# Decoder: six bf16 matmuls of ones in each step and five before the first, whose results nothing reads

## The chip, the cores and the metric

The kernel runs on one core of one Trainium2 chip. The metric is the device time of one execution in microseconds. Three runs of the kernel before took 1675.52, 1684.32 and 1690.44 us (median 1684.32).

## The reference

The program is a chain of eight blocks on an activation `x` of 16 sequences of 64 tokens with 128 features, each adding its result to `x`: an attention decoder with a recurrent cell, three mixture-of-experts blocks, a perceiver, a quantised feed-forward, six transformer layers and one transformer block. The change touches the first one only, the decoder. For each of the 16 sequences, with the normalised tokens as inputs and `cond_1024` as the first hidden state, it computes over 64 steps

```
def step(carry, x):
    h, stopped = carry
    stop = jnp.logical_or(stopped, jnp.mean(x) == 0)
    logits = jnp.concatenate([x, h]) @ W_attn.T + b_attn
    aw = jax.nn.softmax(logits)
    applied = aw @ enc
    comb = jax.nn.relu(jnp.concatenate([x, applied]) @ W_comb.T + b_comb)
    h_new = jnp.tanh(comb @ W_ih.T + b_ih + h @ W_hh.T + b_hh)
    out = h_new @ W_out.T + b_out
```

A step needs the hidden state of the step before it, so the 64 steps cannot be taken in parallel.

## The kernel before

**Layout.** Features stand on the 128 partitions; the 16 sequences are the 16 columns of a step's operands. Whatever does not depend on the hidden state is computed for all steps ahead of the loop (the prologue, L1525 to L1555): `XL`, `XC` and `HX` are the inputs' parts of the logits, of the combination and of the recurrent sum, and `E2` is the context already multiplied by the combination's weights.

**One step** (the loop at L1559) is written in the order in which it runs; the planner that orders other stages is switched off here, so each engine's queue has the order of the source. TensorE works as follows, all in float32:

- `lg`: the step's logits, started by a matmul with the identity that brings in `XL`, and finished by `mm4` with the hidden state. `mm4` (L1334) splits one matmul into four, each of which fills 32 of the array's columns, a column tile. ScalarE takes the exponential into `bd` (L1568).
- `hh`: the recurrent sum, started by an identity matmul that brings in `HX`, continued by `mm4` with `whh` and the old hidden state.
- `su`: the sums of the softmax, `mm4` with ones; VectorE takes the reciprocal.
- `cb`: eight `mm4` of two columns each, the attention applied to `E2`; VectorE multiplies by the reciprocal and takes a maximum, which gives `co` (L1581, L1582).
- `hh` is finished by `mm4` with `wih` and `co`; ScalarE takes the tanh into the next hidden state (L1584).

The identity matmuls of the next step, for `lg` and for `hh`, are issued in this step, ahead of the work on `co` and behind the finishing of `hh`. VectorE gets, at the end of each step, some operations of a list called `todo` (an exact test for inputs of zero mean), which nothing in the loop waits for. PSUM holds two buffers each of `su`, `cb`, `lg` and `hh`, of 16 columns. A float32 matmul stands in the trace as two records, so an `mm4` is eight.

**Matmuls of ones.** `self.units` is a bf16 tile of ones (L1325), and `fill` (L1328) issues n matmuls of it into a PSUM tile that is free. Other stages' planner calls it to keep TensorE occupied; the decoder of the kernel before does not call it. A line in a profile is that of the helper which issues: L296 is every matmul (`mm`), so groups are told apart by tile. After the loop 16 matmuls with `wout` give the block's output (tile `pj` from `H`).

**Around it.** While the prologue and the first steps run, SyncE's queue loads weights of the next stage (`m_sb`, 4 MB in parts), which arrive until about 28.6 us after the span's start. The decoder's steps lie between about 20 and 224.5 us.

Of the kernel before, what the change touches and what calls it, by code (L numbers as in the profile page):

```python
# [13 lines left out]
AF = mybir.ActivationFunctionType  # L14
# [1127 lines left out]
class _Plan:  # L1142
# [122 lines left out]
    def run(self, tries=1, fill=None, banks=()):  # L1265

        for o in reversed(self.ops):
            o.tail = o.ns + max(
                (u.tail + (self.hop(o, u) if full else -o.ns) for u, full in o.users), default=0)
        best = None  # L1270
        for seed in range(tries):
            rng = random.Random(seed)
            shift = {}
            out = self.order(lambda o: 1.0 + (rng.random() - 0.5) * 0.02 * min(seed, 1))
            if out is not None and (best is None or out[-1][1] < best[-1][1]):
                best = out
        fills = self.fills(best, banks) if fill else {}
        for _, _, o, s in best:
            if o.k in fills:
                n, (kind, k) = fills[o.k]  # L1280
                fill(self.kinds[kind][0][k], n)
            if o.takes is not None:
                o.slot = (s, self.kinds[o.takes][0][s])
            o.emit(o.home.slot and o.home.slot[1])
        self.ops = []
        return best


class _Fast(_Net):
# [35 lines left out]
        self.units = self.const.tile([128, 512], BF16, tag="units", name="units")  # L1325
        nc.gpsimd.memset(self.units, 1.0)

    def fill(self, t, n):  # L1328

        t = t[:, 0, :] if len(t.shape) == 3 else t  # L1330
        for _ in range(n):
            self.mm(t, self.units[:, :128], self.units)

    def mm4(self, out, lhsT, rhs, start=True, stop=True):  # L1334

# [174 lines left out]
    def decoder(self):  # L1510
        nc, tc = self.nc, self.tc
        w = self.w0
        x = self.x
        with ExitStack() as st:
            pool = st.enter_context(tc.tile_pool(name="d_sb", bufs=1))
            full = lambda tag: self.tile(pool, [128, B, T], tag)
            H, lnT, XL, XC, HX, RR = (full(k) for k in ("H", "lnT", "XL", "XC", "HX", "RR"))
            E2 = self.tile(pool, [128, NT, D], "E2")
            keep, zero = self.tile(pool, [128, NT], "keep"), self.tile(pool, [128, NT], "zero")
            ones = self.tile(pool, [128, 128], "ones")  # L1520
            nc.gpsimd.memset(ones, 1.0)
            bsum, lbias = self.tile(pool, [128, 1], "bsum"), self.tile(pool, [128, B], "lbias")
            todo = self.exact_zero(pool, x, zero)
            with tc.tile_pool(name="d_ps", bufs=4, space=PSUM) as ps, tc.manual_schedule(engines=None):
                ln = self.tile(pool, [128, NT, D], "ln")  # L1525
                flat = lambda a, h: a[:, h * 8:(h + 1) * 8, :].rearrange("p b t -> p (b t)")
                ctxT = full("ctxT")
                for h in range(2):
                    self.norm_half(x, h, ln[:, h * 4:(h + 1) * 4, :])
                self.to_features(ps, self.ctx, lambda h, t: nc.vector.tensor_copy(flat(ctxT, h), t))  # L1530
                self.to_features(ps, ln, lambda h, t: nc.scalar.copy(flat(lnT, h), t))

                nc.vector.tensor_scalar(lbias, self.c("half16"), -NEG, NEG, ALU.mult, ALU.add)
                nc.vector.tensor_scalar(lbias, lbias, w("battn2"), None, ALU.add)
                nc.vector.tensor_tensor(bsum, w("bih"), w("bhh"), ALU.add)
                for h in range(2):
                    t = self.tile(ps, [128, 512], "pj")
                    self.mm(t, w("wcx"), flat(lnT, h))
                    nc.vector.tensor_scalar(flat(XC, h), t, w("bcomb"), -1.0, ALU.add, ALU.mult)
                for h in range(2):  # L1540
                    t = self.tile(ps, [128, 512], "pj")
                    self.mm(t, w("wax2"), flat(lnT, h))
                    nc.vector.tensor_tensor(
                        XL[:, h * 8:(h + 1) * 8, :], t.rearrange("p (b t) -> p b t", t=T),
                        lbias[:, h * 8:(h + 1) * 8].unsqueeze(2).to_broadcast([128, 8, T]), ALU.add)
                for h in range(2):
                    t = self.tile(ps, [128, 512], "pj")
                    self.mm(t, w("wih"), flat(XC, h))
                    nc.scalar.activation(flat(HX, h), t, AF.Identity, bias=bsum, scale=-1.0)
                for h in range(2):  # L1550
                    t = self.tile(ps, [128, 4, 128], "pj")
                    for k in range(4):
                        i = h * 4 + k
                        self.mm(t[:, k, :], ctxT[:, 2 * i:2 * i + 2, :].rearrange("p b t -> p (b t)"), w("wca"))
                    self.evac(h, E2[:, h * 4:(h + 1) * 4, :], t)  # L1555

            with tc.tile_pool(name="d_rs", bufs=2) as rp, tc.tile_pool(name="d_rps", bufs=2, space=PSUM) as ps, \
                    tc.manual_schedule(engines=None):
                for t in range(T):  # L1559
                    h = w("cond") if t == 0 else H[:, :, t - 1]  # L1560
                    su, cb = (self.tile(ps, [128, 16], k) for k in ("su", "cb"))
                    if t == 0:
                        lg, hh = (self.tile(ps, [128, 16], k) for k in ("lg", "hh"))
                    if t == 0:
                        self.mm(lg, self.ident, XL[:, :, t], True, False)
                    self.mm4(lg, w("wah2"), h, False, True)
                    bd = self.tile(rp, [128, 16], "bd")
                    nc.scalar.activation(bd, lg, AF.Exp)  # L1568
                    if t == 0:
                        self.mm(hh, self.ident, HX[:, :, t], True, False)  # L1570
                    self.mm4(hh, w("whh"), h, False, False)
                    self.mm4(su, ones, bd)
                    r = RR[:, :, t]
                    nc.vector.reciprocal(r, su)
                    for c in range(NT):
                        self.mm4(cb[:, 2 * c:2 * c + 2], E2[:, c, :], bd[:, 2 * c:2 * c + 2])
                    if t < T - 1:
                        lg = self.tile(ps, [128, 16], "lg")
                        self.mm(lg, self.ident, XL[:, :, t + 1], True, False)
                    co = self.tile(rp, [128, 16], "co")  # L1580
                    nc.vector.tensor_tensor(co, cb, r, ALU.mult)  # L1581
                    nc.vector.tensor_tensor(co, co, XC[:, :, t], ALU.max)  # L1582
                    self.mm4(hh, w("wih"), co, False, True)
                    nc.scalar.activation(H[:, :, t], hh, AF.Tanh)  # L1584
                    if t < T - 1:
                        hh = self.tile(ps, [128, 16], "hh")
                        self.mm(hh, self.ident, HX[:, :, t + 1], True, False)
                    for _ in range(-(-len(todo) // (T - t))):
                        todo.pop(0)()
            with tc.tile_pool(name="d_ps2", bufs=2, space=PSUM) as ps:  # L1590

                t = self.tile(ps, [128, 512], "pj")
                self.mm(t[:, :NT], self.c("tri"), zero)
                nc.vector.tensor_scalar(keep, t[:, :NT], 0.5, None, ALU.is_lt)
                out = self.new_x()
                for h in range(2):
                    t = self.tile(ps, [128, 4, 128], "pj")
                    for k in range(4):
                        i = h * 4 + k
                        self.mm(t[:, k, :], H[:, 2 * i:2 * i + 2, :].rearrange("p b t -> p (b t)"), w("wout"))  # L1600
                    o = self.tile(pool, [128, 4, 128], "o", bufs=2)
                    nc.vector.tensor_tensor(o, t, w("bout").unsqueeze(1).to_broadcast([128, 4, 128]), ALU.add)
                    for k in range(4):
                        i = h * 4 + k
                        nc.vector.scalar_tensor_tensor(
                            out[:, i, :], o[:, k, :], keep[:, i:i + 1], x[:, i, :], ALU.mult, ALU.add
                        )
                self.watch(6, RR.rearrange("p b t -> p (b t)"))
        self.x = out
# [924 lines left out]
```

## Time and profile before

| | |
|---|---|
| Median of three runs | 1684.32 us (1675.52 to 1690.44) |
| Profiled execution: time, span | 1676.6 us, 1672.9 us |
| Busy: PE, PEld, DVE, ACT, POOL | 1501.6, 1092.4, 783.3, 536.1, 185.5 us |
| Mean granted TensorE clock over the span | 0.914 |
| Matmuls of ones in other stages (195 into `pj`, 48 into `S`) | 379 ns each (median) |
| Longest standstill of PE in the decoder | 24.62 to 27.85 us |

The profile is of one execution. Times in it are us from the span's start, durations of single instructions ns. PE is TensorE's matmuls, PEld its weight loads, DVE is VectorE, ACT ScalarE, POOL GpSimd. A row of the timeline gives start, duration of the group, engine, line, operation, output and inputs, rows and columns of the array that are in use, shape and type, count, and in brackets the idle time of the engine before it with the work that ended it. Matmuls overlap, so a matmul's duration holds its latency and is longer than its share of the array. The granted clock is the share of full speed that TensorE's array was given.

### The profile page before, as it was taken

How to read it: one execution, taken by the hardware profiler on the slowest of the kernel's cores; microseconds unless marked ns; L12 is line 12 of the kernel's file. 1: busy time of each engine (PE TensorE's matmuls, PEld its weight loads, DVE VectorE, ACT ScalarE, POOL GpSimd, SP SyncE). 2: the span in 40 equal slices, each digit the busy share in tenths (PEclk: the TensorE clock that was granted, in tenths of full speed). 3: DMA queues.
4: the chain of work that ended last, by engine and by line, in shares of the span. 5: the costliest groups of instructions: out<-in, count | busy, mean ns of one | idle time of the engine just before them, and what ended most of it. 6: DMA issues, size and time to landing. Idle time of an engine off the chain costs nothing.

```text
span 1672.9 us, 47624 instructions
## 1 busy us (share of the span) xinstructions
PE 1501.6 (90%) x21466; PEld 1092.4 (65%) x21466; DVE 783.3 (47%) x2505; ACT 536.1 (32%) x885; POOL 185.5 (11%) x227
## 2 busy tenths in 40 slices
PE   6999989999997599998898888888999899999997
PEld 5888856666777246666565656655576677776665
DVE  4435351226334656556676667565311544445112
ACT  2111134432331213424343333434433233332431
POOL 0000010002000032222222122122000101001000
PEclk7555579999999769989999999999999999999999
DMA  6000000000000041000000000000300200000000
GB/s 223 4 5 4 4 2 1 0 1 2 1 2 10 0 175 30 7 25 18 29 17 20 13 20 12 7 16 2 140 2 1 102 2 2 3 2 1 1 1 15
DMA packets 14338, 38.48 MB, mean 23 GB/s; under 512 B 1682, under 2 KB 6674, under 8 KB 14125
## 3 DMA queue, kind: packets, MB, share of 16 engines
q1 hardware_dynamic: 14125, 35.34, 6.2%
q8 instruction: 170, 2.79, 0.7%
q14 instruction: 43, 0.35, 0.1%
HBM read 34.81 MB, written 0.52 MB: 21 GB/s over the span
## 4 chain that ended last, share of the span: by engine, by line
PE 82%; DVE 12%; ACT 3%; issue 2%; DMA 1%; SPq 0%; POOL 0%; ACTq 0%; DVEq 0%
PE pj L296 41%; PE y L296 11%; PE O L296 9%; PE S L296 6%; PE cb L296 3%; PE hh L296 3%; PE lg L296 3%; DVE qx L2373 2%; DVE u L2323 1%; PE pj L1928 1%; ACT P L2451 1%; PE su L296 1%; PE pj L2264 1%; ACT bd L1568 1%; DVE nq L2211 1%
## 5 line engine op out<-in xcount | busy, mean ns | idle before, releaser
L296 PEld LDWEIGHTS y<-m_sb,H 128*128 128x128 f32 x1568 | 188.6, 192 | 57.3 <-issue 35.6
L296 PE MATMUL y<-m_sb,H 128*128 128x128 f32 x1568 | 193.5, 276 | 16.8 <-DVE x L1732 9.8
L296 PE MATMUL pj<-xT,m_sb 128*128 128x512 f32 x392 | 183.8, 598 | 0.0
L2217 POOL TENSOR_TENSOR nq<-nq,minus_half 128x2 f32<-128x2 f32 x120 | 85.2, 715 | 602.1 <-DVE nq L2214 568.5
L2405 ACT ACTIVATE P<-S 128x1024 f32<-128x1024 f32 x96 | 97.9, 1020 | 111.3 <-PE S L296 111.3
L1708 ACT ACTIVATE H<-pj,m_sb 128x512 f32<-128x512 f32 x128 | 87.5, 687 | 132.7 <-PE pj L296 132.4
L1732 DVE SCALAR_TENSOR_TENSOR x<-y,cw,x 128x128 f32<-128x128 f32 x128 | 39.0, 346 | 186.8 <-PE y L296 186.8
L296 PEld LDWEIGHTS pj<-xT,m_sb 128*128 128x128 f32 x392 | 68.9, 191 | 57.4 <-issue 56.9
L2247 ACT ACTIVATE xn<-x,nq 128x128 f32<-128x128 f32 x100 | 48.4, 492 | 152.4 <-DVE nq L2220 142.6
L2323 DVE TENSOR_TENSOR u<-pj,consts_sb 128x512 f32<-128x512 f32 x96 | 66.2, 690 | 35.4 <-PE pj L296 35.0
L1838 DVE COPY QKV<-pj 128x512 f32<-128x512 f32 x56 | 38.7, 691 | 72.5 <-PE pj L296 72.3
L296 PE MATMUL cb<-bd,E 128*32 128x2 f32 x4096 | 65.5, 193 | 3.3 <-issue 3.2
L1708 ACT ACTIVATE H<-pj,b1g,m_sb 128x512 f32<-128x512 f32 x64 | 49.6, 778 | 58.5 <-PE pj L296 55.8
L296 PEld LDWEIGHTS cb<-bd,E 128*32 128x32 f32 x4096 | 62.9, 156 | 3.5 <-issue 3.3
L296 PE MATMUL pj<-xT,w_sb 128*128 128x512 f32 x128 | 63.0, 611 | 1.4 <-DVE xT L2292 1.4
L296 PE MATMUL pj<-xT,l_f 128*128 128x512 f32 x96 | 50.4, 618 | 11.9 <-ACT P L2451 11.8
L1895 ACT ACTIVATE P<-S 128x1024 f32<-128x1024 f32 x32 | 32.8, 1024 | 85.0 <-PE S L296 84.7
L1732 DVE SCALAR_TENSOR_TENSOR acc<-y,cw,acc 128x128 f32<-128x128 f32 x64 | 19.5, 346 | 86.5 <-PE y L296 86.5
L296 PE MATMUL pj<-units 128*128 128x512 bf16 x195 | 55.7, 396 | 4.5 <-DVE x L2079 1.9
L1584 ACT ACTIVATE H<-hh 128x16 f32<-128x16 f32 x64 | 12.9, 202 | 138.8 <-PE hh L296 138.8
L296 PEld LDWEIGHTS O<-QKV,P 64*64 64x64 f32 (+1 forms) x1536 | 48.7, 135 | 13.2 <-issue 5.3
L296 PE MATMUL O<-QKV,P 64*64 64x65 f32 (+1 forms) x1536 | 55.2, 222 | 2.0 <-DVE On L1923 1.8
(363 smaller groups left out, 2738.9 us busy)
## 6 DMA issues: line engine op xcount, KB each, us to landing
w_sb<-in_w SPq DMA_DIRECT2D x7, 681.5 KB, 8.3
m_sb<-in_m SPq DMA_DIRECT2D x8, 515.0 KB, 7.6
m_sb<-in_m SPq DMA_DIRECT2D x8, 514.5 KB, 5.9
m_sb<-in_m SPq DMA_DIRECT2D x7, 565.5 KB, 9.3
l_f<-in_l SPq DMA_DIRECT2D x6, 578.5 KB, 3.9
l_a<-in_l SPq DMA_DIRECT2D x6, 387.0 KB, 3.1
l_s<-in_l SPq DMA_DIRECT2D x6, 384.0 KB, 3.2
w_sb<-in_w SPq DMA_DIRECT2D x4, 512.5 KB, 11.7
```

The costliest lines, as they stand in the source:

```text
L296: self.nc.tensor.matmul(out, lhsT=lhsT, rhs=rhs, start=start, stop=stop, **kw)
L1568: nc.scalar.activation(bd, lg, AF.Exp)
L1708: nc.scalar.activation(a[:, c, :], ups[c].slot[1], act, bias=b, scale=g)
L1732: nc.vector.scalar_tensor_tensor(acc[:, k, :], src, g, x0[:, i, :] if first else acc[:, k, :], ALU.mult, ALU.add)
L1838: e(o, i.rearrange("p (b t) -> p b t", t=T) if len(o.shape) == 3 else i)
L1895: P = plan.op("ACT", 1030, lambda P, S=S: nc.scalar.activation(P.rearrange("p (j n) -> p j n", j=2), S.slot[1], AF.Exp, scale=0.125), [o f ...
L1928: t = plan.op("PE", 700, lambda t, On=On: [nc.tensor.transpose(t[:, i * 128:(i + 1) * 128], On.slot[1][:, i * 128:(i + 1) * 128], self.ide ...
L2217: return lambda t: nc.gpsimd.tensor_tensor(t[:, :, b], t[:, :, a], self.minus_half[:, 0:2], ALU.pow)
L2247: nc.scalar.activation(o, xk[:, i, :], AF.Identity, bias=f[1], scale=f[0])
L2323: us.append(plan.op("DVE", 690, lambda u, t=t, k=k, table=table: nc.vector.tensor_tensor(view(u[:, k, :]), view(t.slot[1]), self.c(table). ...
L2373: nc.vector.tensor_scalar(o, r, m, None, ALU.mult)
L2405: P = plan.op("ACT", 1030, lambda P, S=S: nc.scalar.activation(P.rearrange("p (g c) -> p g c", g=4), S.slot[1][:, :, 0:256], AF.Exp, scale ...
```

## The change

`fill` gets an argument `start`, which it hands to the matmul as both flags (with `False` the matmul adds to what stands in PSUM and opens or closes no group), and takes as many columns of ones as its target has. Five fills of 512 columns stand behind the prologue. The `lg` and `hh` tiles grow from 16 to 512 columns, the first 16 of which hold what they held; each step has two fills of 480 columns in each of three places, into columns 32 to 511: behind `hh`'s `whh` part, behind the next step's identity matmul of `lg`, and behind that of `hh`. The last step has only the first pair. The identity matmuls of step 0, for `lg` and `hh`, both move ahead of the loop. ScalarE and VectorE run the same instructions as before, in the same order.

```diff
-    def fill(self, t, n):
+    def fill(self, t, n, start=True):
         t = t[:, 0, :] if len(t.shape) == 3 else t
         for _ in range(n):
-            self.mm(t, self.units[:, :128], self.units)
+            self.mm(t, self.units[:, :128], self.units[:, :t.shape[1]], start, start)
...
+                self.fill(self.tile(ps, [128, 512], "pj"), 5)
...
+                def started(tag, src, t):
+                    p = self.tile(ps, [128, 512], tag)
+                    self.mm(p[:, 0:16], self.ident, src[:, :, t], True, False)
+                    return p
+
+                lg, hh = started("lg", XL, 0), started("hh", HX, 0)
                 for t in range(T):
                     h = w("cond") if t == 0 else H[:, :, t - 1]
                     su, cb = (self.tile(ps, [128, 16], k) for k in ("su", "cb"))
-                    if t == 0:
-                        lg, hh = (self.tile(ps, [128, 16], k) for k in ("lg", "hh"))
-                    if t == 0:
-                        self.mm(lg, self.ident, XL[:, :, t], True, False)
-                    self.mm4(lg, w("wah2"), h, False, True)
+                    self.mm4(lg[:, 0:16], w("wah2"), h, False, True)
                     bd = self.tile(rp, [128, 16], "bd")
-                    nc.scalar.activation(bd, lg, AF.Exp)
-                    if t == 0:
-                        self.mm(hh, self.ident, HX[:, :, t], True, False)
-                    self.mm4(hh, w("whh"), h, False, False)
+                    nc.scalar.activation(bd, lg[:, 0:16], AF.Exp)
+                    self.mm4(hh[:, 0:16], w("whh"), h, False, False)
+                    self.fill(hh[:, 32:512], 2, False)
                     self.mm4(su, ones, bd)
...
                     if t < T - 1:
-                        lg = self.tile(ps, [128, 16], "lg")
-                        self.mm(lg, self.ident, XL[:, :, t + 1], True, False)
+                        lg = started("lg", XL, t + 1)
+                        self.fill(lg[:, 32:512], 2, False)
...
-                    self.mm4(hh, w("wih"), co, False, True)
-                    nc.scalar.activation(H[:, :, t], hh, AF.Tanh)
+                    self.mm4(hh[:, 0:16], w("wih"), co, False, True)
+                    nc.scalar.activation(H[:, :, t], hh[:, 0:16], AF.Tanh)
                     if t < T - 1:
-                        hh = self.tile(ps, [128, 16], "hh")
-                        self.mm(hh, self.ident, HX[:, :, t + 1], True, False)
+                        hh = started("hh", HX, t + 1)
+                        self.fill(hh[:, 32:512], 2, False)
```

## The prediction

> **What bounds the kernel now.** I read the page's sliced row first, then the busy times of chosen stretches, then single steps of the decoder in the order of time.
>
> ```profile
> PE   6999989999997599998898888888999899999997
> PEclk7555579999999769989999999999999999999999
> ```
>
> Each digit is 1/40 of the span (41.8 us). TensorE looks busy throughout, but in slices 2 to 5, the decoder's, the granted clock is half.
>
> ```profile
> 27.85:221.90 194.05, 178.94 (x6215) 160.43 (x6215) 80.83 (x362) 24.12 (x126) 0.00 (x0) 0.50 0.02 5
> ...
> 1088.10:1091.50 3.40, 1.77 (x6) 0.78 (x6) 2.92 (x13) 0.99 (x2) 1.24 (x2) 1.00 0.34 133
> 1310.00:1313.40 3.40, 1.28 (x6) 0.39 (x4) 2.99 (x22) 0.92 (x3) 3.28 (x6) 1.00 1.03 419
> ```
>
> The numbers after the stretch are its length, then busy us of PE, PEld, DVE, ACT, POOL, then the granted clock. From 27.85 on the clock is 0.50 for 194 us. The other two are 3.4 us stretches at full clock in other stages; after the second one the clock falls. One step at full clock (the first), all engines:
>
> ```profile
> 20.45 0.26 PE L296 MATMUL lg<-w_sb 128*32 128x16 f32 x8
> 20.82 0.18 ACT L1568 ACTIVATE bd<-lg 128x16 f32<-128x16 f32 x1 [0.75 <-PE lg L296]
> 21.89 0.40 PE L296 MATMUL lg<-XL,consts_sb 128*128 128x16 f32 x2
> 22.47 0.26 PE L296 MATMUL hh<-co,w_sb 128*32 128x16 f32 x8 [0.19 <-DVE co L1582]
> 22.66 0.40 PE L296 MATMUL hh<-HX,consts_sb 128*128 128x16 f32 x2
> 22.80 0.20 ACT L1584 ACTIVATE H<-hh 128x16 f32<-128x16 f32 x1 [1.79 <-PE hh L296]
> 23.05 0.31 PE L296 MATMUL lg<-H,w_sb 128*32 128x16 f32 x8
> ```
>
> and one at half clock:
>
> ```profile
> 101.41 0.31 PE L296 MATMUL lg<-H,w_sb 128*32 128x16 f32 x8
> 102.08 0.31 PE L296 MATMUL su<-bd,ones 128*32 128x16 f32 x8 [0.25 <-ACT bd L1568]
> 103.15 0.61 PE L296 MATMUL lg<-XL,consts_sb 128*128 128x16 f32 x2
> 103.74 0.31 PE L296 MATMUL hh<-co,w_sb 128*32 128x16 f32 x8
> 103.98 0.61 PE L296 MATMUL hh<-HX,consts_sb 128*128 128x16 f32 x2
> 104.52 0.31 PE L296 MATMUL lg<-H,w_sb 128*32 128x16 f32 x8
> ```
>
> The step is one chain: lg, exp, su and cb, the two DVE operations, hh, tanh, lg again. It takes 3.11 us at half clock (101.41 to 104.52). At full clock: lg to exp 0.37, exp to su 0.23 (101.85 to 102.08 in the slow step), su (21.12) to the identity matmul 0.77, on to hh 0.58, to tanh 0.33, to lg 0.25, together 2.53 us. So the clock is worth 0.58 us a step, 37 us in 64. The question is what the fills take of it.
>
> **What the Trainium skill says.** "TensorE: Matmul & The Clock Gate", Part 1 (What's actually happening): the array's clock is half or full, chosen from activity in free-running windows of 3413 ns. The trace agrees: only 0.50 and 1.00 occur within a window, and the decoder stays at 0.50. Same page, Back-to-back issue gap: a warm 512-column matmul follows the last by about 216 ns; here 21 of them take 4.69 us at 379 ns each, so (4.69-0.38)/20 = 0.2156. Same page, Part 3 (What overlaps and what doesn't): a weight load passes running matmuls only where row groups differ. The fills use all 128 rows, as the decoder's column tiles do, and the trace shows the consequence:
>
> ```profile
> 229.64 4.69 PE L296 MATMUL pj<-units 128*128 128x512 bf16 x21 [1.18 <-DVE o L1602]
> ...
> 675.34 0.39 PE L296 MATMUL pj<-units 128*128 128x512 bf16 x1
> ...
> 675.65 0.26 PEld L296 LDWEIGHTS O<-Vc,P 128*64 128x64 f32 x6 [0.23 <-issue]
> ```
>
> After one fill, the weight load of a column-tiled matmul, waiting for nothing, starts 0.32 us after the fill's start (677.02 after 676.70 likewise): 0.21 of streaming and 0.105 of drain.
>
> **The change part by part, at full clock.** A fill of 480 columns streams 480/512 x 0.2156 = 0.202 us. A pair followed by a column tile holds the array 0.20 + 0.20 + 0.105 = 0.51 us from its start. No engine but PE gets work, no DMA is moved, and no instruction inside the loop gets a new wait; so the only cost is that the next matmul finds PE occupied.
>
> *Pause 1*, after whh, for exp: lg and whh start their last of 16 passes about 0.16 after lg; going from column tiles to the full array takes 0.11 (last hh pass at 22.47+0.26-0.18 = 22.55, identity at 22.66). Fills 0.27 to 0.78. su is ready at 0.37+0.23 = 0.60. Late by 0.18.
>
> *Pause 2*, after the lg identity, for co: the identity's two weight loads lie 0.11 apart, the fill's own follows; I take its matmul 0.25 after the identity's start (0.33, the distance 22.66+0.33 to a column tile as at 20.12 to 20.45, is the upper end). Fills 0.25 to 0.76; hh was ready at 0.58. Late by 0.17.
>
> *Pause 3*, after the hh identity, for tanh: identity 0.19 after hh, fills at 0.44 to 0.95; lg was ready at 0.33+0.25 = 0.58. Late by 0.37. This "pause" at full clock is only 0.15 us long once the identity is through.
>
> Step: 2.53+0.18+0.17+0.37 = 3.25; I take 3.24. Against 3.11 that is +0.13, in 62 steps **+8.1 us**. The bounds of the unknowns: 3.15 if half of the drains is hidden, 3.32 if the identity needs 0.33.
>
> *Does the clock hold?* I count streaming, as full-clock time: 0.42 ns per bf16 column (0.2156/512), twice that per f32 pass. Counted so from the shapes, the 1088 stretch has 0.375 of its length and holds, the 1310 stretch 0.353 and loses the clock; at half clock the stretch at 224.6 with 0.40 regains it, and one at 586 with 0.344 (its 88 rows counted as 88/128) doesn't. The limit is near 0.36 to 0.375. A step of fills has 6x0.202 + 0.59 of its own (32 passes of 16 columns in column tiles, 4 in identities, 64 of 2) = 1.80 in 3.24: 0.55, safe; with the column tiles counted by a quarter still 0.43.
>
> *But the clock falls once anyway.* PE stands still from 24.62 to 27.85 with no releaser, while the loads move some 400 GB/s; one packet of the instruction queue lands in that time, so I read it as PE out of instructions. The fills don't remove it, and 3.2 us of idling empties at least one window. Then fills run at half clock: pairs of 0.80 plus drain make the lateness about 0.6, 0.8 and 0.85, the step 5.3 to 5.5 us. Its mean density is 1.80/5.3 = 0.34, but the best 3.4 us of it (pause 2 to pause 1 of the next step) have 0.40 to 0.42, so some window soon regains the clock. About 11 us (range 6 to 28) at half clock, each costing 1-3.24/5.3 = 0.39: **+4.3 us** (2 to 11).
>
> *Before the first step.* Five fills of 0.2156 start when E2's matmuls end (about 19.3), under the copies of E2 that end at 20.08 and that lg waits for anyway; the last completes about 20.6, and both identities now stand before lg (0.33 more). Some 0.75 later, partly swallowed by the standstill: **+1.0** (0 to 2). *After the last step* the 16 output matmuls (225.03 to 228.46) run at full clock; DVE's chain behind them then starts earlier: **-1.2** (-1.7 to 0).
>
> Sum: 8.1+4.3+1.0-1.2 = **+12.2 us**. The profiled execution has a span of 1672.9 and a time of 1676.6, 7.7 below the median of 1684.32; a difference within the span carries over, so 1684.3+12.2 = **1696 us** (1684 to 1712).
>
> **The rivals.** *Stuck at half clock* (slower): if a column tile counts by its 32 of 128 columns, the best window of a cold step has only 0.33 to 0.35, below the limit, and the fills that were to lift the clock lengthen every step: 62 x (5.3-3.11) = +136, with the start +137: 1821; with luck in the windows anything from 1730 to 1835. It decides at density 0.36. For it: the O tiles of 64 columns make the limit uncertain. Against: windows rich in those hold the clock at an area-weighted 0.315. *Fills fit the pauses* (faster): if drains and half of a pair's streaming overlap the latency of the next tile, a step is 2.8: 62 x (2.8-3.11) = -19, and with +2 for the start -17: 1667 (1656 to 1682). For it: 0.35 and 0.33 us of pauses 1 and 2 are nearly as long as a pair. Against: pause 3 and the measured 0.32. *Clock gain and fill cost cancel* (or the fills change nothing): 1684.
>
> **How the numbers follow.** Chances: forecast 0.56, stuck 0.20, fit 0.18, cancel 0.06. This kernel's measurement tells about 1%, 17 us, from no change. Within it lie 0.7 of the forecast (0.40), cancel (0.06) and a sixth of fit (0.03): 0.49. Faster 0.15; slower 0.16+0.20 = 0.36. The range 1656 to 1725 leaves out nearly all of stuck and the tails.
>
> **What would show it.** The clock at 1.00 from some 35 to 45 us on; steps of 3.24; the fill pairs 0.20 apart; su, hh and lg no longer waiting for ACT and DVE but for PE; the output matmuls at 275 ns instead of 421. Wrong if a step is under 3.1 (the drain or the pauses mis-sized) or 0.50 stays in slices 2 to 5 (the window's count).

## The result and the profile after

The changed kernel takes 1709.99 us in the median of 20 runs (1689.98 to 1722.42), the kernel before 1684.18 in the median of 20 (1675.52 to 1691.32): 25.8 us or 1.5% slower. The ratio is 1.0129, 95% interval [1.0102, 1.0155], some 22 us; it leaves out every run more than 1.5% above the fastest of its kernel and so lies a little below the ratio of the medians. The forecast was 1696 with a range of 1656 to 1725. The profiled execution has a span of 1701.0 us and a time of 1703.27.

The sliced rows of the page:

```profile
PE   7999999998999489888898989888999899999997
PEclk9999989999999769999999999999999999999999
```

The half clock that filled slices 2 to 5 is gone in this execution. The busy times of three stretches, from shortly before the first step to the decoder's end (length, then busy us of PE, PEld, DVE, ACT and POOL, the granted clock, the DMA share, GB/s):

```profile
20.00:30.90 10.90, 8.24 (x224) 4.96 (x222) 2.92 (x13) 1.35 (x5) 0.00 (x0) 1.00 0.83 243
30.90:37.70 6.80, 6.80 (x126) 3.26 (x124) 1.12 (x6) 0.57 (x3) 0.00 (x0) 0.50 0.01 2
37.70:236.00 198.30, 197.92 (x6404) 118.36 (x6404) 76.95 (x350) 23.19 (x122) 0.00 (x0) 1.00 0.02 4
```

In the last one PE is busy for 197.92 of 198.30 us: from 37.7 on TensorE is the bound of the decoder. One step, in the order of time:

```profile
99.91 0.33 PE L296 MATMUL lg<-H,w_sb 128*32 128x16 f32 x8
...
100.26 0.58 PE L296 MATMUL hh<-units 128*128 128x480 bf16 x2
100.33 0.18 ACT L1574 ACTIVATE bd<-lg 128x16 f32<-128x16 f32 x1 [0.82 <-PE lg L296]
...
100.77 0.26 PE L296 MATMUL su<-bd,ones 128*32 128x16 f32 x8
...
101.52 0.39 PE L296 MATMUL lg<-XL,consts_sb 128*128 128x16 f32 x2
...
101.76 0.56 PE L296 MATMUL lg<-units 128*128 128x480 bf16 x2
101.86 0.19 DVE L1587 TENSOR_TENSOR co<-co,XC 128x16 f32<-128x16 f32 x1
...
102.25 0.26 PE L296 MATMUL hh<-co,w_sb 128*32 128x16 f32 x8
...
102.58 0.20 ACT L1589 ACTIVATE H<-hh 128x16 f32<-128x16 f32 x1 [2.06 <-PE hh L296]
102.68 0.56 PE L296 MATMUL hh<-units 128*128 128x480 bf16 x2
...
103.18 0.33 PE L296 MATMUL lg<-H,w_sb 128*32 128x16 f32 x8
```

The step is 3.27 us (99.91 to 103.18). The exponential ends at 100.51 and `su` starts at 100.77; `co` ends at 102.05, `hh` starts at 102.25; the tanh ends at 102.78, `lg` starts at 103.18. No PE row carries a bracket of idle time. From the first fill of a pair to the next column tile there are 0.51, 0.49 and 0.50 us.

The standstill during the load is still there, with the clock's fall after it. At the other end the last step, which has no second and third pair of fills, loses the clock as well:

```profile
26.08 0.50 PE L296 MATMUL cb<-bd,E 128*32 128x2 f32 x36
29.14 0.42 PE L296 MATMUL cb<-bd,E 128*32 128x2 f32 x28 [2.56 <-issue]
...
235.70 0.73 PE L296 MATMUL cb<-bd,E 128*32 128x2 f32 x64
...
238.81 0.26 PE L296 MATMUL hh<-co,w_sb 128*32 128x16 f32 x8 [2.38 <-DVE co L1587]
```

The decoder's last tanh starts at 224.34 before and at 239.14 after, +14.8 us. The rest of the profiles' difference, 13.4 us, lies behind it, where the programs are the same and this execution spent more time at half clock. How much half clock an execution has can be worked out for every run, profiled or not, as 2 x (1 - mean clock) x span: here 2 x 0.038 x 1701.0 = 129 us, of which 6.8 in the decoder and 122 behind it; in the profile of before 288 us, of which 205 in the decoder and 83 behind it.

### The profile page after: what moved, and what is told of

It is laid out like the page before. It is cut to its first block, busy times and chain, and to the rows that moved or that the text cites. A ratio compares the mean times of both kernels' runs of the same rounds, so it can differ in the third digit from the quotient of the medians.

```text
span 1701.0 us, 48394 instructions
## 1 busy us (share of the span) xinstructions
PE 1546.0 (91%) x21851; PEld 1063.1 (62%) x21851; DVE 783.1 (46%) x2505; ACT 536.0 (32%) x885; POOL 185.4 (11%) x227
## 4 chain that ended last, share of the span: by engine, by line
PE 84%; DVE 11%; ACT 2%; issue 2%; DMA 1%; SPq 0%; POOL 0%; DVEq 0%; ACTq 0%
PE pj L296 42%; PE y L296 11%; PE O L296 9%; PE S L296 6%; PE hh L296 6%; PE lg L296 4%; PE cb L296 2%; DVE qx L2378 2%; PE pj L1933 1%; DVE u L2328 1%; ACT P L2456 1%; PE pj L2269 1%; PE su L296 1%; PE pj L2429 1%; DVE nq L2216 1%
## 5 line engine op out<-in xcount | busy, mean ns | idle before, releaser
L296 PEld LDWEIGHTS <-units 128*128 128x128 bf16 x628 | 59.5, 117 | 36.5 <-issue 13.7
L296 PE MATMUL hh<-units 128*128 128x480 bf16 x254 | 74.0, 373 | 0.0
L1579 DVE RECIPROCAL RR<-su 128x16 f32<-128x16 f32 x64 | 16.7, 260 | 107.7 <-PE su L296 107.7
L296 PE MATMUL pj<-units 128*128 128x512 bf16 x200 | 59.8, 412 | 4.2 <-DVE x L2084 1.9
```

Source lines behind the costliest of these rows:

```text
L296: self.nc.tensor.matmul(out, lhsT=lhsT, rhs=rhs, start=start, stop=stop, **kw)
```

## The experiments

All kernels are edits of the changed kernel unless said otherwise. "Half clock" is time at granted clock 0.50. The kernel before, run beside them, had these medians: 1681.34 with the kernels of 32 rows, of four and two fills and without the load; 1683.37 with the load spread, the second profile, the 16 fills and the fills as column tiles; 1683.38 with the other three. Each ratio is to the kernel before beside it.

**What counts towards the clock: fills of 32 rows, and fewer fills.** The first kernel reads only 32 of the 128 rows in the loop's fills. Nothing else changes.

```diff
-            self.mm(t, self.units[:, :128], self.units[:, :t.shape[1]], start, start)
+            r = 128 if start else 32
+            self.mm(t, self.units[:r, :128], self.units[:r, :t.shape[1]], start, start)
```

> The decoder's fills use 32 of the array's 128 rows; their number, columns and places are those of the changed kernel. Theory (the clock follows streaming weighted by rows; the step is bound by TensorE's occupation): the fills count a quarter, the clock stays at 0.50 through the decoder, a step takes 5.3 to 5.5 us and the whole kernel about 1820 us. Rival (any occupation of the array lifts the clock): clock 1.00 and steps of 3.27 us as in the changed kernel, about 1710 us.

Measured: 1832.77 us, one run. A long stretch of its decoder:

```profile
25.80:360.00 334.20, 331.83 (x6404) 178.82 (x6404) 77.97 (x355) 23.44 (x123) 0.00 (x0) 0.50 0.02 5
```

PE is busy for 331.83 of 334.20 us, with the same instructions as the changed kernel (6404 in both stretches), and the clock stays at 0.50; steps are 5.47 us. So neither busy time nor the number of columns that stream is what counts; the rows in use count. The run also gives the price of the rival that was forecast as "stuck at half clock" with 1821 us.

Two kernels have six fills in the first 12 steps, to bring the clock up, and then four or two:

```diff
-                        self.fill(hh[:, 32:512], 2, False)
+                        self.fill(hh[:, 32:512], 2 if t < 12 else 0, False)
```

That is the third pause (four fills are left); the kernel with two has `2 if t < 12 else 1` in the other two pauses besides.

> No fills behind the hh identity from step 12 on; steps 0 to 11 as in the changed kernel, so that the clock is back at full by then. Theory: a step drops from 3.27 to 2.90 us (the 0.37 of the third pause goes), streaming is (4x0.202+0.59)/2.90 = 0.48 of the time and the clock holds; 51 x 0.37 = 19 us less than the changed kernel, about 1691 us. Rival (column tiles count by their width, a quarter): 0.33, the clock falls and the step goes to about 4.5 us, over 1750 us.

> From step 12 on one fill in each of the first two pauses and none in the third. Theory (column tiles count in full): the fills fit the pauses (0.27+0.20+0.105 = 0.58 against 0.60, 0.25+0.20+0.105 = 0.56 against 0.58), the step is 2.55 us, streaming (2x0.202+0.59)/2.55 = 0.39, just above the limit of 0.36 to 0.375, and the clock holds: 51 x 0.72 = 37 us less than the changed kernel, about 1673 us. Rival (four column tiles that stream at once count once, or by width): 0.29 or less, the clock falls at about step 13 and stays down, the step is some 3.7 us and the whole about 1732 us.

Measured: four fills 1755.8 us (1731.7 to 1761.8, 4 runs), ratio 1.036 [1.0251, 1.0469]; two fills 1726.24 (1715.42 to 1741.91, 4 runs), ratio 1.0299 [1.0218, 1.038]. Stretches of the decoder, first of four fills, then of two:

```profile
77.00:105.00 28.00, 27.39 (x940) 17.70 (x940) 8.80 (x54) 3.43 (x18) 0.00 (x0) 1.00 0.02 4
107.00:290.00 183.00, 183.00 (x4265) 113.11 (x4264) 52.43 (x230) 15.78 (x82) 0.00 (x0) 0.50 0.01 3
```

```profile
53.00:76.80 23.80, 23.07 (x795) 14.33 (x794) 10.08 (x43) 2.67 (x14) 0.00 (x0) 1.00 0.02 4
76.80:268.00 191.20, 188.40 (x5141) 139.82 (x5142) 66.92 (x295) 19.42 (x101) 0.00 (x0) 0.50 0.02 4
```

With four fills the step at full clock took 2.92 us (2.90 was expected), for a few steps; then the clock fell and steps of 4.47 us followed to the end. With two it fell at once, to steps of 3.67. Both came close to the rivals that were named for them (steps of 4.5 and 3.7 us). Counted by streaming with the column tiles in full, the four-fill step has (4 x 0.202 + 0.59)/2.92 = 0.48, far above the limit of 0.36 to 0.375; counted by a quarter (0.59 becomes about 0.19) it has 0.34, below it. The clock wasn't held, so my count of the column tiles was too high. Counted by a quarter the six-fill step has (1.21 + 0.19)/3.27 = 0.43 at full clock.

A quarter is too little, though. In each trace all changes of the clock lie whole multiples of 3.41 us apart, so they show where the windows lie. Here the clock fell at 106.2, and the last window at full clock is 102.8 to 106.2. It holds a short standstill with no releaser:

```profile
104.42 0.22 PE L296 MATMUL cb<-bd,E 128*32 128x2 f32 x2 [0.41 <-issue]
```

Worked out from its records, it has 0.39 to 0.41 with the column tiles in full and 0.27 to 0.29 by a quarter. The window from 85.7 to 89.1 has 0.42 and 0.30, and the clock stayed. The stretch at 1310 of the kernel before, which has no column tiles and which the prediction counts at 0.353, lost it. So a column tile counts for less than its whole streaming and for more than a quarter of it; how much is not settled here.

**Where the fall comes from.** In the first kernel here the next block's weights `m_sb` are set to zero instead of loaded: it leaves that load out, and the block behind the decoder works on zeros.

```diff
-            self.nc.sync.dma_start(out=t[:, a:b], in_=src[:, a:b])
+            if name == "m0":
+                self.nc.gpsimd.memset(t[:, a:b], 0.0)
+            else:
+                self.nc.sync.dma_start(out=t[:, a:b], in_=src[:, a:b])
```

In the second the load stays, in eight parts, each of which waits for decoder step 1, 7, 13 and so on, through a column that VectorE copies in the step and GpSimd writes into the part's place.

```diff
+            if name == "m0" and getattr(self, "gates", None) is not None:
+                k = a // step
+                self.nc.gpsimd.tensor_copy(t[:, a:a + 1], self.gates[:, k:k + 1])
...
+                    if t % 6 == 1 and t // 6 < 8:
+                        nc.vector.tensor_copy(self.gates[:, t // 6:t // 6 + 1], co[:, 0:1])
```

> The changed kernel without the load of the next block's 4 MB of weights (they are set to zero, so that block adds nothing; the decoder is untouched). Theory (the load starves TensorE of instructions, the standstill of about 3 us drops the clock): no standstill, the clock stays at 1.00 from the prologue to the decoder's end, steps of 3.27 us from the first on, the decoder 5 to 6 us shorter. Rival (the standstill has another cause): it stays, with the fall of the clock behind it.

> The changed kernel with the next block's load issued in eight parts, each released by a step of the decoder (steps 1, 7, 13 and so on), so that it does not come in one burst ahead of the first steps. Theory: no standstill and no fall of the clock, the decoder lasts as in the run without the load (last tanh near 234 to 236 us), some 15 us less than the changed kernel's median, about 1695 us, with a narrower spread; still slower than the kernel before by the fills' cost. Rival (the re-entry costs the predicted 4 us only): about 1704 us.

Measured: without the load 1692.9 us, one run; with the load spread 1688.11 (1681.75 to 1697.96, 13 runs), ratio 1.0029 [1.0003, 1.0056]. In both the standstill is gone, and the clock doesn't fall in the decoder before its last step. Without the load, then with it spread:

```profile
30.00:230.00 200.00, 199.65 (x6448) 119.34 (x6448) 77.34 (x347) 23.39 (x122) 0.00 (x0) 1.00 0.02 4
```

```profile
24.40:230.00 205.60, 205.06 (x6594) 122.35 (x6594) 80.18 (x363) 23.99 (x126) 1.99 (x8) 1.00 0.09 27
```

With the load spread, the 64 `cb` matmuls in which the changed kernel stood still for 2.56 us run through:

```profile
25.93 0.73 PE L299 MATMUL cb<-bd,E 128*32 128x2 f32 x64
```

So the burst of the load makes the standstill. That the fall comes from the standing still, and not from the transfers themselves, is supported by the changed kernel's last step, where PE stands still for 2.38 us and the clock falls though the DMA engines moved nothing from 235.7 to 239.1. The spread kernel is 22 us under the changed one and still 5 us (by the ratio 0.03 to 0.56%) over the kernel before: with the clock held nearly throughout, the fills still cost a little more than the clock gives.

The same spread of the load in the kernel *before* (no fills) says what it is worth by itself:

> The kernel before with the load of the next block's weights in eight parts that decoder steps 1, 7, 13 and so on release; no fills. Theory: this takes out the standstill of 3.2 us and nothing else, the steps stay at half clock and 3.11 us, so some 3 us less than before, about 1680 us; the same spread of the load in the changed kernel gave 1688, so the steady cost of the fills alone, all at full clock, is then 7 to 9 us. Rival: the fills' steady cost is nil and the spread load itself costs something (parts that arrive late, or a copy on VectorE in the chain): then this kernel is at 1686 to 1690 us, level with the changed kernel with its load spread.

Measured: 1681.2 us (1675.68 to 1690.51, 22 runs), ratio 0.9989 [0.997, 1.0008]. The standstill is gone; the steps stay at half clock, most of them 3.11 us:

```profile
27.18 0.31 PE L299 MATMUL su<-bd,ones 128*32 128x16 f32 x8 [0.24 <-ACT bd L1572]
27.31 1.01 PE L299 MATMUL cb<-bd,E 128*32 128x2 f32 x64
```

The 64 `cb` matmuls run through where the kernel before stopped for 3.2 us. The gain of some 2 us can't be told from none. With the load spread in both, the fills cost 1688.11 - 1681.2 = 6.9 us; by the two ratios 6.7, with an uncertainty of some 5. In the two profiles the last tanh starts at 221.65 without fills and at 233.83 with them, 12.2 us apart.

**How the clock comes back.** The changed kernel was profiled a second time, and a kernel with 16 instead of 2 fills in the first pause of step 2 was run, to fill one window for certain:

```diff
-                    self.fill(hh[:, 32:512], 2, False)
+                    self.fill(hh[:, 32:512], 16 if t == 2 else 2, False)
```

> The changed kernel once more, for a second profile. Theory (the excess over the prediction is time at half clock behind the standstill, which the free-running windows make long or short, and luck with the windows in the later stages): steps of 3.27 us as before, but another length at half clock in the decoder, anything from 7 to 45 us, each costing 0.4 us, and another length of what follows the decoder between 1447 and 1464 us. Rival (each execution is alike and the later stages are slower because of the change): 7 us at half clock again and 1462 us behind the decoder.

> Step 2, the first behind the standstill, has 16 fills in its first pause in place of 2: 14 x 0.40 = 5.6 us more at half clock, a solid train that fills a window wherever it lies. Theory: the clock is back within two or three windows in every execution, so the long returns of 20 to 45 us vanish; the median is near 1705 us, and the slowest runs are below 1715. Rival (the spread comes from the later stages): 5 us slower than the changed kernel, about 1715, with the same spread up to 1725.

Measured: the changed kernel again, 1705.92 us, with these stretches:

```profile
28.80:69.80 41.00, 41.00 (x777) 21.39 (x777) 12.71 (x54) 3.26 (x18) 0.00 (x0) 0.50 0.01 3
69.80:236.00 166.20, 166.20 (x5389) 99.56 (x5388) 61.84 (x291) 19.26 (x101) 0.00 (x0) 1.00 0.02 4
```

This time it took 41.0 us at half clock, not 6.8, with seven steps of 5.27 us, until the clock came back. Behind the last tanh it took 1453.4 us, with 95 us at half clock, where the first profile had 1461.9 and 122: the rival that the change makes the later stages slower is not borne out. With the 16 fills: 1703.92 us (1690.37 to 1707.01, 10 runs), ratio 1.0107 [1.0074, 1.0141], and 6.8 us at half clock in the profiled execution. Half clock of whole runs, worked out as above, with a straight line through the spans of each kernel's runs:

| kernel | runs | half clock, median (range), us | span by the line, us | span at 118 us of half clock |
|---|---|---|---|---|
| changed | 20 | 150 (101 to 182) | 1648.2 + 0.398 per us | 1695.2 |
| with the 16 fills | 10 | 122 (91 to 126) | 1647.3 + 0.438 per us | 1699.0 |
| load spread | 13 | 108 (84 to 129) | 1648.8 + 0.366 per us | 1692.0 |

The correlations are 0.98, 0.98 and 0.96: nearly all of the scatter of a kernel's runs goes with the time that it spends at half clock. At equal half clock the changed kernel is 3.2 us above the one with the load spread, about the length of the standstill (2.56 and 2.85 in its two profiles). The 16 fills save 28 us of half clock in the median, about 11 us, and cost some 4 of their own; the medians differ by 6.1. With them no run has more than 126 us of half clock, where the changed kernel has up to 182. So the coming back is dear, and its length differs from one execution to the next; a solid train of fills makes it short.

**Is there a cheaper form?** Three tries. Five fills instead of six (one in the third pause), with the load spread:

```diff
-                        self.fill(hh[:, 32:512], 2, False)
+                        self.fill(hh[:, 32:512], 1, False)
```

> The changed kernel with the spread load and one fill instead of two in the third pause, five a step. Theory (a column tile counts by a quarter): the step's share of streaming is (5 x 0.202 + 0.19)/3.07 = 0.39, above the limit of 0.36 to 0.375, so the clock holds, the step is 0.20 us shorter, 3.07 us, and the time 12 us under the kernel with six fills and spread load, about 1676. Rival: a window of 3.4 us that holds the stretch with one fill twice has only 0.35; the clock falls within the loop, steps of 4.8 to 4.9 us follow, and the time is 1700 to 1770.

Measured: 1725.29 us in the median, but 1679.63 to 1781.17 in six runs. The profiled execution is the fastest:

```profile
24.00:224.00 200.00, 195.41 (x6594) 122.20 (x6593) 81.77 (x365) 24.00 (x126) 2.00 (x8) 1.00 0.09 28
```

There the clock held and the step was 3.07 us, as expected, with some of 3.2 to 3.9 between. The other five runs had 191 to 395 us of half clock instead of 97, which is the rival. Whether a kernel this near the limit holds the clock differs from one execution to the next. Six fills are the fewest of those tried with which the runs hold together.

The loop's fills and identity matmuls as four column tiles each (spread load), to avoid switches between column tiles and the full array:

```diff
-            self.mm(t, self.units[:, :128], self.units[:, :t.shape[1]], start, start)
+            (self.mm if start else self.mm4)(t, self.units[:, :128], self.units[:, :t.shape[1]], start, start)
...
-                    self.mm(p[:, 0:16], self.ident, src[:, :, t], True, False)
+                    self.mm4(p[:, 0:16], self.ident, src[:, :, t], True, False)
```

> As the kernel with the load in eight parts, but each loop fill is four column tiles of 32 columns (480 bf16 columns of data each, streaming at once), and the identity matmuls are issued as four column tiles as well, so that the array never changes between the full form and column tiles inside the loop. Theory (the change of form costs 0.105 us behind each pair and 0.11 ahead of it, and the identity in the full form 0.33): pairs of 0.405 us fit all three pauses or nearly, the step falls from 3.27 to 2.55 to 2.75 us; four tiles at once count as one full matmul, (1.21+0.15)/2.6 = 0.5, the clock holds; 64 x 0.6 = 38 us less than its counterpart, about 1655 us, and so faster than the kernel before. Rival (four column tiles count as one tile, a quarter, or do not stream at once): the clock falls and steps take 4 us or more, over 1740 us.

Measured: 1719.56 us (1714.41 to 1729.13, 4 runs), ratio 1.0235 [1.0186, 1.0285]. A miss: steps of 3.9 us in the mean. The clock mostly held, but PE stood still about once a step with nothing to wait for:

```profile
25.00:267.00 242.00, 179.18 (x8508) 111.56 (x8508) 85.56 (x368) 23.81 (x124) 2.15 (x8) 0.95 0.08 24
```

```profile
100.69 0.24 PE L299 MATMUL hh<-HX,consts_sb 128*32 128x16 f32 x4
102.91 0.21 PE L299 MATMUL hh<-HX,consts_sb 128*32 128x16 f32 x2 [1.99 <-issue]
```

And the kernel before with the load spread and only its two identity matmuls a step as column tiles, no fills:

```diff
-                        self.mm(lg, self.ident, XL[:, :, t + 1], True, False)
+                        self.mm4(lg, self.ident, XL[:, :, t + 1], True, False)
...
-                        self.mm(hh, self.ident, HX[:, :, t + 1], True, False)
+                        self.mm4(hh, self.ident, HX[:, :, t + 1], True, False)
```

> As the run above, and the two identity matmuls of a step as four column tiles each, so that the array is never switched between column tiles and full width. Theory: at half clock the step loses the switches that lie in its chain, the two of 0.11 to 0.25 us around the identity for hh, and is 2.95 to 3.0 us long: 62 x 0.13 = 8 us less than the run above. Rival: the twelve additional passes of each step reach the rate at which TensorE can be supplied with instructions (it stood still 1 to 2.3 us a step in the kernel with all fills as column tiles), steps of 3.1 us or more and no gain or a loss.

Measured: 1686.18 us (1678.02 to 1691.76, 14 runs), ratio 1.0001 [0.9984, 1.0019]: no gain.

```profile
31.94 0.94 PE L299 MATMUL cb<-bd,E 128*32 128x2 f32 x57
33.51 0.23 PE L299 MATMUL cb<-bd,E 128*32 128x2 f32 x4 [0.63 <-issue]
```

```profile
30.00:220.00 190.00, 133.35 (x6649) 109.83 (x6643) 80.55 (x349) 22.65 (x119) 2.15 (x7) 0.50 0.09 27
```

A step without a standstill is 2.96 us, so the two identity matmuls in the full form, with the switches around them, do cost 0.15; but the mean of the first 62 steps is 3.19. Both kernels run into the same thing at nearly the same mean rate: (8508 + 8508)/242 = 70.3 PE instructions per us in the first, (6649 + 6643)/190 = 70.0 in the second, where the kernel before has (6215 + 6215)/194.05 = 64.1 and the changed one 64.6, neither with more than stray standstills of this kind. It isn't a hard rate: over 20 us the first has (788 + 784)/20 = 78.6 (58.1 to 78.1). No version was found that is measurably faster than the kernel before.

## Why the prediction was right, and which term was too small

The terms of its sum against the runs, in us:

| term | forecast | measured |
|---|---|---|
| 62 steps, full clock with fills for half clock without | +8.1 (step 3.24) | +9.9 (3.27 - 3.11 = 0.16 each) |
| back from half clock after the standstill | +4.3 (11 us, 6 to 28) | about +16 (42 us in the median) |
| before the first step | +1.0 | +1.7 and +0.7 (first tanh at 24.53 and 23.48 in the two profiles, before 22.80) |
| standstill itself | unchanged | -0.7 and -0.4 (2.56 and 2.85, before 3.23) |
| output matmuls | -1.2 | 0 |
| sum | +12.2 | about +26; difference of the medians +25.8, by the ratio some 22 |

The two small rows are within what executions differ by: a kernel without fills (the last one above) has its first tanh at 24.37.

*The steady step: right.* The 0.51 us for which a pair of fills holds the array was measured as 0.51, 0.49 and 0.50. The signs named came: `su`, `hh` and `lg` behind PE instead of ACT and DVE, and the clock at 1.00 from 37.7 on in the first profile. The kernel with the load spread shows the same 3.27 from its first step on. "Fills fit the pauses" falls with it. The spread pair of kernels gives less for the whole, 6.9 us, than this row and the start do together (10.6 to 11.6); its two profiles give 12.2 at the last tanh, and the uncertainty of some 5 us leaves room for both.

*The clock holds with six fills: right, for a count that was too generous.* I took 0.55 with column tiles in full, and 0.43 with a quarter as the careful end. The four-fill kernel shows that the truth lies between them. "Safe" was too much said: one fill fewer lost the clock in five of six runs.

*The failing step is the re-entry: "the best 3.4 us of it have 0.40 to 0.42, so some window soon regains the clock", 11 us.* The fall itself and its cause were right. But that count had the column tiles in full. Three pairs of fills that follow each other in a half-clock step of the second profile:

```profile
45.00 0.96 PE L296 MATMUL lg<-units 128*128 128x480 bf16 x2
...
46.58 0.96 PE L296 MATMUL hh<-units 128*128 128x480 bf16 x2
...
47.83 0.98 PE L296 MATMUL hh<-units 128*128 128x480 bf16 x2
```

Each pair streams for 0.80 us, so the third ends 3.63 us after the first began. The best 3.41 us hold 0.58 + 0.80 + 0.80 us of half-clock streaming, 1.09 at full clock, with 0.08 for 24 column-tile records counted by a quarter and 0.03 for the identity: 1.20/3.41 = 0.35. That is the count that the rival "stuck" gave, and it lies just at the limit (0.353 to 0.375 by the prediction's own fit). So the kernel neither comes back soon nor stays down: profiled were 6.8 and 41.0 us, and the kernels with fewer fills, whose first 12 steps are the same, add 47.8 and 23.9. Two of the four lie in the forecast's range of 6 to 28. By the whole runs, the median of the changed kernel has 150 us of half clock, and the kernel that has none in its profiled decoder before the last step 108; the 42 us between are the decoder's share, if the later stages have the same in both. This is an estimate from those two medians. At 1 - 3.27/5.27 = 0.38 each that is 16 us, 12 more than forecast; the forecast missed by 14. The Trainium skill ("TensorE: Matmul & The Clock Gate", Part 1, What's actually happening) says: "The warm-up budget is ~3.4 µs of time, not a number of matmuls." Here PE was busy for 41.00 of 41.00 us before the clock came back: it takes a window with enough streaming, and PE's busy time doesn't tell that.

The traces let the windows be counted one by one, because the four stretches at half clock are 2, 12, 14 and 7 times 3.41 us. With each matmul's streaming set at the start of its record, the window after which the clock came back is the fullest of its stretch in all four: 0.35 to 0.36 by a quarter, against at most 0.34 in any window before it. With the column tiles in full these are 0.42 to 0.43, against at most 0.415. So windows as full as the "0.40 to 0.42" of the prediction did pass without bringing the clock back; it took the second, the twelfth, the fourteenth and the seventh window. With the 16 fills it came back after a window of 0.51. The working depends a little on where in its record a matmul streams (0.15 us later, the order changes in one of the four).

It also shows that the count in full was wrong: behind the decoder of the kernel with the load spread, the window from 235.6 to 239.0, which has no column tiles, brought the clock back with 0.37 to 0.40, while windows of 0.41 in full, in three of the four profiles, did not.

*The end: wrong, by little.* The output matmuls still take 421 ns. The last step has no fills after its first pair, and VectorE's two reductions keep `co` back, so PE stands still for 2.38 us and the clock falls as the last tanh starts. That wait was in the trace before:

```profile
223.96 0.31 PE L296 MATMUL hh<-co,w_sb 128*32 128x16 f32 x8 [2.11 <-DVE co L1582]
```

I passed over it.

*The size of the effect.* I held "within 1%" (0.49) a little likelier than "slower by over 1%" (0.36). With 11 us of re-entry it would have been within; with 42 it isn't. That the measured time lies inside the range owes more to the width of the range than to the sum, which has 12 of the 26 us. The profiled execution has little half clock in the decoder and much in later stages (6.8 and 122 us); the second profile has more in the decoder and less behind it (41 and 95), and the times are close (1703.27, 1705.92). A comparison of these two profiles by stage alone would have put the cost in the wrong place.

## What to carry to other kernels

Fills that hold a clock must be priced on the chain that they interrupt: here the clock was worth 0.58 us a step (3.11 - 2.53, by the one step at full clock), and the fewest fills found that hold it reliably cost 0.74 (3.27 - 2.53). Count for both states whether a window reaches the limit, at full clock to stay and at half clock to come back; a kernel that holds its clock only just, or can regain it only just, has times that scatter by 2 to 6%. Where a program with a clock like this scatters, set each run's span against its time at half clock before reading stages off one profile.

## What the runs showed of the hardware that was not expected

- A column tile of 32 columns counts towards the clock for less than its streaming in full: at half clock a window of 0.41 so counted didn't bring the clock back, while one of 0.37 to 0.40 without column tiles did. It counts for more than its share of the array, a quarter: a window of 0.30 so counted kept the clock. 480-column fills as four column tiles at once mostly held it (0.95 over 242 us).
- Rows count too: with fills of 32 rows the clock was at 0.50 for 355 us, with PE busy for 331.83 of 334.20 us of it. This is one run.
- TensorE stood still for 0.6 to 2.4 us at a time with no releaser in the two kernels that asked for the most matmuls and weight loads; their mean rates were 70.3 and 70.0 per us, where those of 64 to 65 ran with hardly a standstill. A burst of loads did the same for 2.6 to 3.2 us at once; with the load in eight parts it didn't happen. The traces don't name the mechanism; that TensorE runs out of instructions, and that their own transfers are the limit, is an inference. If it is right, the step of 2.53 us that the forecast took for full clock without fills, with its 200 PE instructions (79 per us), may not be one that can be kept up: the most that these traces show over 20 us is about that.
